# Layer 0's end put into an explicit order, and ranks read from rows with VectorE's 32x32 block transposes

## The chip, the cores and the metric

The kernel runs on one core of one Trainium2 chip. Its time is the device time in microseconds (us) of one execution. Besides the timed runs there is one execution taken by the hardware profiler; all views of the profile come from it. Engines: PE is TensorE's matmul, PEld its weight load, DVE is VectorE, ACT is ScalarE, POOL is GpSimd, SP is SyncE, which issues most of the transfers.

## The reference

Four graph layers over N = 2708 nodes with 128 features and one dense float32 adjacency matrix A. Each adds its result to x after a layer norm and a ReLU.

```
h = relu(layernorm(x))
# layer 0: degrees, a first product, the four nearest nodes, a second product
d  = 1/sqrt(rowsum(A));  z = leaky_relu((d * (A @ (d*h))) @ W1 + b1, 0.1)
S  = exp(-|z_i - z_j| / 2), kept for the 4 largest of each row, else 0
A2 = S + A;  d2 = 1/sqrt(rowsum(A2));  x += (d2 * (A2 @ (d2*h))) @ W2 + b2
# layer 1: attention
XW = h @ W;  Z = leaky_relu(s_row[:,None] + s_col[None,:], 0.01);  den = exp(Z)
att = den / (A @ den);  x += A @ (att @ XW)
# layer 2
x += h @ W_self + (A @ h / clip(rowsum(A), 1)) @ W_neigh
# layer 3
x += relu((A @ h) @ K + bias)
```

Here s_row and s_col are products of XW with the two halves of a vector.

## The kernel before, in words

**Tiles.** The nodes are T = 22 tiles of 128, the last one (T-1) with TAIL = 20 rows. A arrives transposed; a chunk is one tile of its rows, 128 x 2708 float32, 1354 KB. Columns of a product are cut into NKB = 6 blocks (`KBS`, five of 512 and one of 148), which are also the six groups of tiles (`GROUPS`). PSUM has six accumulators `acc(0)` to `acc(5)` and two small buffers `ps`. Chunks go through four `big` buffers and five `res` buffers, the latter for the last five tiles.

**Order of the work.** The program is written in order, but a scheduler chooses the order on each engine; `pin` fixes an instruction in program order among the pinned ones. SP issues the chunk loads in program order (they are pinned), and each waits until its buffer is free.

**Layer 0.** First the column sums of the chunks are taken on PE, with the layer norm's products `weighted` between them. `aggregate(y1, to_z)` is the first product with A. Each strip of similarities (one tile against all nodes) is then computed on PE, copied by ACT, and searched by DVE with MAX8 and FIND_INDEX8. For the last four strips (`LATE = T - 4`) the index is looked up later, in `find_last`. From the similarities come `dinv2`, the scaled rows `y2`, and their copy in DRAM, `ydr`, from which `add_near` gathers each tile's four neighbours: one indirect DMA of POOL for each of the four, and one DVE instruction that adds it to `xs`.

The second product is `aggregate(y2, done_l0)`: 17 chunks stream, then the tail, then the five resident chunks block by block. After a block is complete, `done_l0` turns it (`to_x1`), adds it to x, normalizes, adds late neighbours and computes terms of layer 1. `r_nat` holds one number for each node in the layout of the tiles, `row_all` the same numbers as a row on all partitions.

**Layer 1's ranks.** Node j's rank is the count of nodes i with `r_i >= r_j` and i before or at j in the order of ties. `place(t)` compares tile t with the nodes behind it (`mask`), counts by matmuls with ones into rows of `cnt`, and treats the tile's own 128 columns apart (`own_tiles`: less-or-equal minus ties under the diagonal). The remaining count (`later`) comes from a sum over the mask on ACT or DVE. `places_of(b)` brings a group's counts from a row of `cnt` to partitions: a copy, then four matmuls with a single partition, into `cn`. POOL scatters the group's nodes to `order_d` with one indirect DMA per tile. Between these, `total` multiplies each chunk by `w_n`; 9 chunks are resident then, 13 are loaded again. The sorted list `srtT` is loaded and turned on PE, and `fetch` gathers rows of A in this order by indirect DMA for the knots, a running sum over sorted rows, written to `table` in DRAM. Then rows are fetched from `table`, interpolated, and multiplied. Layers 2 and 3 are further calls of `aggregate`.

Of the kernel before, what the change touches and what calls it, by code (L numbers as in the profile page):

```python
# [25 lines left out]
def kernel(  # L26
# [46 lines left out]
    def pin(ins):  # L73

        return tc.keep_in_program_order(ins)

# [99 lines left out]
    one_b = ones_b[:, 0:1]  # L176
# [20 lines left out]
    def acc(b):  # L197
        return ps_a.tile([P, 512], F32, name=f"acc{b}")

# [166 lines left out]
    for i in range(T):  # L366
        c = chunk(i)
        w = width(i)
        if 3 <= i < 3 + 3 * NG:
            weighted((i - 3) // 3, i % 3)  # L370
        for b, (k0, n) in enumerate(KBS):
            g = 32 * (b % 4)
            nc.tensor.matmul(
                sums[b // 4][g : g + 32, :n],
                ones[:w, :32],
                c[:w, k0 : k0 + n],
                start=(i == 0),
                stop=(i == T - 1),
            )
        if i < FIRST:  # L380
            del resident[i]
    sum_rows = lay.tile([P, 1024], F32, name="sum_rows", tag="U")
# [112 lines left out]
    LATE = T - 4  # L495
# [3 lines left out]
    def strip(t):  # L499
        if LATE <= t < LATE + 2:  # L500
            return lay.tile([P, N], F32, name=f"strip{t}", tag="UZ"[t - LATE])
# [67 lines left out]
    nc.scalar.activation(dinv2, deg2s, AF.Exp, scale=-0.5)  # L569
    y2 = lay.tile([P, T, D], F32, name="y2", tag="Y")  # L570
    ydr = dram.tile([P * T, D], F32, name="ydr")
    for i in range(2):
        resident[i] = chunk(i)
    for t0, t1 in ((0, T // 2), (T // 2, T)):
# [14 lines left out]
    for t in (T - 2, T - 1, *range(LATE, T - 2)):  # L589
        find_last(t)  # L590
# [9 lines left out]
    def add_near(t, late=False):  # L600
        w = width(t)
        for k in range(TOPK):
            g = res.tile([P, D], F32, name="gath", bufs=23)
            nc.gpsimd.indirect_dma_start(  # L604
                out=g[:w, :],
                out_offset=None,
                in_=ydr[:, :],
                in_offset=bass.IndirectOffsetOnAxis(ap=near_u[:w, t, k : k + 1], axis=0),
            )
            term = nc.vector.scalar_tensor_tensor(  # L610
                xs[:w, t, :],
                g[:w, :],
                simd[:w, t, k : k + 1],
                xs[:w, t, :],
# [3 lines left out]
            if late and k == 0:  # L618
                pin(term)
# [34 lines left out]

# [20 lines left out]
    def last_terms(g):  # L675

        t0, t1 = GROUPS[g]
        k0, n = KBS[g]
        prod = res.tile([P, 4, D], F32, name="prod")
        nc.vector.tensor_tensor(  # L680
# [4 lines left out]
        )  # L685
        e = min(t1, T - 1)
        nc.vector.tensor_reduce(r_nat[:, t0:e], prod[:, : e - t0, :], AX.X, ALU.add)
        if e < t1:
            nc.vector.tensor_reduce(
                r_nat[:TAIL, e:t1], prod[:TAIL, e - t0 : t1 - t0, :], AX.X, ALU.add  # L690
            )
        p = ps_s.tile([P, 512], F32, name="ps")
        for t in range(t0, t1):
            w = width(t)
            o = (t - t0) * P
            nc.tensor.transpose(
                p[:, o : o + w], r_nat[:w, t : t + 1].to_broadcast([w, P]), ident[:w, :w]
            )
        return nc.scalar.copy(row_all[:, k0 : k0 + n], p[:, :n])
# [13 lines left out]
    def own_tiles(g, pool):  # L713
        t0, t1 = GROUPS[g]
        for c0, c1, w in ((t0, min(t1, T - 1), P), (max(t0, T - 1), t1, TAIL)):
            n = c1 - c0
            if n <= 0:
# [3 lines left out]
            eq = pool.tile([P, 4, P], BF16, name="eq", tag="spare")[:w, :n, :w]  # L721
            pin(nc.vector.tensor_tensor(eq, rows_, mine, ALU.is_equal))
            nc.vector.tensor_tensor(
                eq, eq, tri[:w, None, :w].to_broadcast([w, n, w]), ALU.mult
            )
            o = own[:w, c0:c1, :w]
            nc.vector.tensor_tensor(o, rows_, mine, ALU.is_le)
            nc.vector.tensor_tensor(o, o, eq, ALU.subtract)


    late = {0: (15,), 1: (16,), 2: (17,), 3: (18, 19), 4: ()}

    def done_l0(g, s2):
        to_x1(g, s2)
        if g < NG - 1:
            layernorm_relu(h1, g)
            for t in late[g]:
                add_near(t, late=True)
        if 1 <= g < NG - 1:
            terms(g - 1)  # L740
        if g == NG - 1:
            last_terms(g - 1)
        if g > 2:
            column_terms(g - 3)
        if g in (2, 3):
            own_tiles(g - 2, res)
# [3 lines left out]
    aggregate(y2, done_l0, lambda i: spread(y2, nc.sync) if i == 4 else None, kept=4)  # L750
    transposed(hT, h1, NG - 2, nc.scalar.copy)
    column_terms(NG - 3)
    for t in range(GROUPS[-1][0], T):
        add_near(t, late=True)
    layernorm_relu(h1, NG - 1)
    last_row = last_terms(NG - 1)
    transposed(hT, h1, NG - 1, nc.scalar.copy)
    column_terms(NG - 2)
# [17 lines left out]
    cnt, cn = (acc(2), acc(3)), (acc(4), acc(5))  # L776
# [10 lines left out]
    rmax = node_max("rmax", r_nat, r_ps[0][:, 256:384])  # L787
    r_n = vec("r_n")
# [24 lines left out]
    def place(t):  # L813
# [4 lines left out]
        def count(mask, c0, c1, first):  # L818
# [5 lines left out]
                ones_b[:w, :32],  # L824
                mask,
                start=(t == 0 and first),
                stop=(c1 == e and c1 in (512 * b + 512, N)),
            )

        count(own[:w, t, :w], a, e, True)  # L830
        if e < N:
            mk = flags.tile([P, N], BF16, name="mask")
            if t in (2, 6):
                nc.vector.tensor_scalar(
                    mk[:w, e:],
                    row_all[:w, e:],
                    rt,
                    0.0,
                    op0=ALU.is_le,
# [538 lines left out]
```

## Time and profile before

| | us |
|---|---|
| timed, median of 3 | 1194.0 |
| timed, lowest to highest | 1188.3 to 1194.6 |
| profiled execution, own time | 1289.2 |
| its span | 1287.3 |
| PE busy in the span | 1056.8 |
| DVE busy | 561.4 |
| ACT busy | 409.7 |
| POOL busy | 245.7 |
| mean granted TensorE clock | 0.902 of full speed |

The page gives busy time by engine, then the span in 40 slices, DMA queues, the chain that ended last and the costliest groups of instructions. A busy PE is not PE at its peak: a float32 matmul is two passes, and each pass takes twice as long at half clock. A timeline row has its start, its duration, the engine, the line in the code, the operation with output and inputs, and in brackets how long the engine had been idle and what ended that ("issue" is nothing that the profile shows). A table of stretches has, for each, the length, the busy time of PE, PEld, DVE, ACT and POOL with counts, the granted clock, the DMA engines' share and GB/s.

### The profile page before, as it was taken

The numbers are of one execution on the slowest core, as the hardware profiler recorded it, in microseconds if no ns is written. First come the engines' busy times: TensorE is split into PE (matmuls) and PEld (weight loads), VectorE is DVE, ScalarE is ACT, GpSimd is POOL, SyncE is SP. The second block draws the span as 40 slices with busy tenths as digits, with TensorE's granted clock in tenths as the row PEclk, the third lists the DMA queues.
The fourth block names the chain that finished last, engine by engine and source line by source line (L and its number), as shares of the span: only waits on it lengthen the run. The fifth ranks groups of instructions, "written<-read, shape, count | busy, mean of one in ns | idle before, by whom it ended". The sixth has DMA issues, their size and how long they took to land. (4 is left out here: it accounts for less than half of the span.)

```text
span 1287.3 us, 10181 instructions
## 1 busy us (share of the span) xinstructions
PE 1056.8 (82%) x3603; PEld 499.3 (39%) x3603; DVE 561.4 (44%) x1177; ACT 409.7 (32%) x636; POOL 245.7 (19%) x211
## 2 busy tenths in 40 slices
PE   4879999999763379797677771787879999999998
PEld 1324444444221134454333330333334445545444
DVE  2020026999832001783466663899970012104003
ACT  3100014544300000475567644687840012003000
POOL 4000000000277700134211103577500000000000
PEclk9989999999875579788899896698889999999999
DMA  9997800001553361256999997999949945761841
GB/s 344 422 383 276 302 3 1 1 1 43 212 202 96 94 253 50 90 233 245 274 406 395 345 348 269 423 414 419 417 184 395 326 164 181 265 245 54 306 159 43
DMA packets 38800, 298.76 MB, mean 232 GB/s; under 512 B 6735, under 2 KB 9710, under 8 KB 12290
## 3 DMA queue, kind: packets, MB, share of 16 engines
q1 hardware_dynamic: 24798, 203.76, 42.0%
q0 software_dynamic: 13952, 94.36, 19.7%
q8 instruction: 28, 0.46, 0.1%
q14 instruction: 22, 0.18, 0.0%
HBM read 265.76 MB, written 32.87 MB: 232 GB/s over the span
## 5 line engine op out<-in xcount | busy, mean ns | idle before, releaser
L284 PE MATMUL acc<-chunk,y 128*128 128x512 f32 (+1 forms) x408 | 180.3, 591 | 74.7 <-issue 58.4
L1213 PE MATMUL acc<-hi,xw 128*128 128x512 f32 (+3 forms) x264 | 124.2, 634 | 57.8 <-DVE hi L1203 57.8
L1106 PE MATMUL acc<-mov,wt 128*128 128x512 f32 (+1 forms) x264 | 115.4, 592 | 40.7 <-DMA mov<-in_adj_dram,src_u 39.2
L284 PE MATMUL acc<-chunk,h 128*128 128x512 f32 (+1 forms) x384 | 148.3, 542 | 0.0
L604 POOL DMA_INDIRECT gath<-ydr,near_u x88 | 83.8, 952 | 337.5 <-DMA ydr<-y 245.9
L284 PEld LDWEIGHTS acc<-chunk,y 128*128 128x128 f32 x408 | 79.5, 205 | 175.5 <-issue 162.0
L512 PE MATMUL acc<-zT 128*128 128x512 f32 (+2 forms) x264 | 112.7, 559 | 0.4 <-ACT strip L527 0.3
L1213 PEld LDWEIGHTS acc<-hi,xw 128*128 128x128 f32 (+1 forms) x264 | 55.7, 220 | 126.3 <-issue 66.1
L1110 DVE COPY mov<-acc 2x512 f32<-2x512 f32 x126 | 74.3, 611 | 61.1 <-PE acc L1106 60.5
L284 PEld LDWEIGHTS acc<-chunk,h 128*128 128x128 f32 x384 | 68.6, 190 | 73.2 <-issue 73.1
L1106 PEld LDWEIGHTS acc<-mov,wt 128*128 128x128 f32 x264 | 52.1, 205 | 103.8 <-issue 82.3
L527 ACT COPY strip<-acc 128x512 f32<-128x512 f32 (+2 forms) x132 | 60.7, 556 | 61.0 <-issue 35.8
L284 PE MATMUL acc<-chunk,attended 128*128 128x512 f32 x192 | 73.1, 542 | 2.5 <-DMA chunk<-in_adj_dram 2.5
L1145 POOL DMA_INDIRECT lo<-table,lo_u x22 | 58.0, 2638 | 68.6 <-issue 41.1
L1111 ACT COPY knots<-acc 128x512 f32<-128x512 f32 x88 | 50.2, 590 | 62.9 <-DVE mov L1110 56.4
L1195 ACT ACTIVATE hi<-hi,lam 128x2708 f32<-128x2708 f32 (+3 forms) x24 | 56.5, 2363 | 35.6 <-issue 26.7
L1191 DVE SCALAR_TENSOR_TENSOR hi<-lo,lam,hi 128x2708 f32<-128x2708 f32 (+3 forms) x24 | 67.1, 2801 | 1.0
L1203 DVE SCALAR_TENSOR_TENSOR hi<-row_all,inv_s,hi 128x2708 f32<-128x2708 f32 (+3 forms) x24 | 67.0, 2797 | 0.4 <-ACT hi L1196 0.4
L512 PEld LDWEIGHTS acc<-zT 128*128 128x128 f32 (+1 forms) x264 | 45.0, 185 | 51.7 <-issue 41.9
L529 DVE MAX8 top_v<-strip 128x8 f32<-128x2708 f32 (+1 forms) x22 | 64.4, 2967 | 0.4 <-ACT strip L527 0.4
L650 ACT COPY u2T<-acc 128x512 f32<-128x512 f32 (+1 forms) x6 | 3.2, 533 | 168.3 <-PE acc L284 168.2
L1196 ACT ACTIVATE hi<-hi,hb 128x2708 f32<-128x2708 f32 (+3 forms) x24 | 56.5, 2361 | 0.7
(281 smaller groups left out, 1179.5 us busy)
## 6 DMA issues: line engine op xcount, KB each, us to landing
chunk<-in_adj_dram SPq DMA_DIRECT2D x108, 1354.0 KB
table<-knots SPq DMA_DIRECT2D x20, 1354.5 KB
res<-in_adj_dram SPq DMA_DIRECT2D x9, 1354.0 KB
chunkY<-in_adj_dram SPq DMA_DIRECT2D x2, 1354.0 KB
chunkU<-in_adj_dram SPq DMA_DIRECT2D x2, 1354.0 KB
res<-in_adj_dram SPq DMA_DIRECT2D x8, 211.6 KB
ydr<-y SPq DMA_DIRECT2D x2, 704.0 KB
gath<-ydr,near_u POOLq DMA_INDIRECT x88
```

Of the source, the lines that this page charges most:

```text
L284: nc.tensor.matmul(out[b][:, :n], y[r, i, :], chunk(i)[r, k0 : k0 + n], start=(i == 0), stop=(i == T - 2),)
L512: mm = nc.tensor.matmul(zz[b][:w, :n], zT[:, cols(t)], zT[:, k0 : k0 + n], start=True, stop=False)
L527: copied = nc.scalar.copy(s[:w, k0 : k0 + n], zz[b][:w, :n])
L529: nc.vector.max(top_v[:w, t, :], s[:w, :])
L604: nc.gpsimd.indirect_dma_start(out=g[:w, :], out_offset=None, in_=ydr[:, :], in_offset=bass.IndirectOffsetOnAxis(ap=near_u[:w, t, k : k + ...
L1106: nc.tensor.matmul(p[:, :n], wt[:, t, :], moving[t][:, k0 : k0 + n], start=True, stop=True)
L1110: nc.vector.tensor_copy(moving[t + 1][:2, k0 : k0 + n], p[:2, :n])
L1145: nc.gpsimd.indirect_dma_start(out=dst[:w, :], out_offset=None, in_=table[:, :], in_offset=bass.IndirectOffsetOnAxis(ap=idx[:w, t : t + 1] ...
L1191: nc.vector.scalar_tensor_tensor(num, lo[:w, c], kap, num, op0=ALU.mult, op1=ALU.add)
L1195: nc.scalar.activation(num, num, AF.Ln, scale=sc)
L1203: nc.vector.scalar_tensor_tensor(att[:w, c], row_all[:w, c], inv_s[:w, t : t + 1], att[:w, c], op0=ALU.max, op1=ALU.mult,)
L1213: nc.tensor.matmul(py[b][:, :n], xw[:w, t, :], att[:w, k0 : k0 + n], start=(t == T - 1), stop=(t == T - 2),)
```

## The change

It has these parts.

- `warm` issues bf16 matmuls of 128x512 whose result nobody reads: three after each of the last six chunks of the sums, 16 ahead of the second product, 14 ahead of the knots. In the sums the 20-row tile T-1 goes before T-2.
- `LATE` is T-5. Three of the late strips take the places of resident chunks 17 to 19, which are loaded again during the second product; four chunks instead of two are loaded ahead of it. `ydr` is written in three parts.
- Layer 0's end is written out through `Ordered`, which pins every instruction of PE, DVE and ACT: the last two blocks are completed first, and then turned, added and normalized in one sequence. The 20-row tile's neighbours come from one gather on four strips of partitions, added up by one matmul. Its indices and factors are spread by eight small DMAs on ACT's queue. Groups 3, 4 and 5 get their terms by row sums on DVE, and are transposed after the maximum of `r_nat`.
- `own_tiles` has two instructions instead of four, and keeps only the ties. `place` compares from the tile's own columns on, and takes the ties off by a matmul with minus one.
- `places_of` uses four 32x32 block transposes on DVE per group instead of the copy and the matmuls.
- Two `total` fewer stand between the counts.

```diff
+    def warm(p, n):
+        for _ in range(n):
+            pin(
+                nc.tensor.matmul(
+                    p, ident_b, ident_b[:, None, :].to_broadcast([P, 4, P]), start=True, stop=True
+                )
+            )
...
-    for i in range(T):
+    for n_, i in enumerate([*range(T - 2), T - 1, T - 2]):
...
+        if n_ >= T - 6:
+            warm(acc(0), 3)
...
-    LATE = T - 4
+    LATE = T - 5
...
     def strip(t):
-        if LATE <= t < LATE + 2:
-            return lay.tile([P, N], F32, name=f"strip{t}", tag="UZ"[t - LATE])
+        if t in (LATE, T - 2, T - 1):
+            i = T - L0_RES + (LATE, T - 2, T - 1).index(t)
+            del resident[i]
+            return res_rows.tile([P, N + 1], F32, name=f"strip{t}", tag=f"res{i}")[:, :N]
+        if t > LATE:
+            return lay.tile([P, N], F32, name=f"strip{t}", tag="UZ"[t - LATE - 1])
...
+    warm(acc(5), 16)
...
-    for i in range(2):
+    for i in range(4):
         resident[i] = chunk(i)
-    for t0, t1 in ((0, T // 2), (T // 2, T)):
+    for t0, t1 in ((0, 9), (9, 17), (17, T)):
...
+    for k in range(TOPK):
+        for dst, src in ((near_p, near_u), (simd_p, simd)):
+            nc.scalar.dma_start(dst[32 * k : 32 * k + TAIL, :], src[:TAIL, T - 1, k : k + 1])
...
+    def last_near():
+        g = gathered(near_p)
+        dve.tensor_scalar(four_w, four_w, simd_p, None, op0=ALU.mult)
+        p = ps_s.tile([P, 512], F32, name="ps")
+        pe.matmul(p[:TAIL, :P], four_w[:, :TAIL], g, start=True, stop=True)
+        return p
...
-            pin(nc.vector.tensor_tensor(eq, rows_, mine, ALU.is_equal))
-            nc.vector.tensor_tensor(
-                eq, eq, tri[:w, None, :w].to_broadcast([w, n, w]), ALU.mult
-            )
             o = own[:w, c0:c1, :w]
-            nc.vector.tensor_tensor(o, rows_, mine, ALU.is_le)
-            nc.vector.tensor_tensor(o, o, eq, ALU.subtract)
+            pin(nc.vector.tensor_tensor(o, rows_, mine, ALU.is_equal))
+            nc.vector.tensor_tensor(o, o, tri[:w, None, :w].to_broadcast([w, n, w]), ALU.mult)
...
     def done_l0(g, s2):
+        if g >= NG - 2:
+            complete.append(s2[g])
+            return
         to_x1(g, s2)
-        if g < NG - 1:
-            layernorm_relu(h1, g)
-            for t in late[g]:
-                add_near(t, late=True)
...
+    column_terms(0)
+    add_near(T - 3, dve)
+    x1(E4)
+    for t in range(*GROUPS[E4]):
+        moments(t)
+    roots(E4)
+    x1(E5)
+    normed(E4)
+    p = last_near()
+    prod = row_sums(E4 - 1)
+    natural(E4 - 1, prod)
+    as_row(E4 - 1)
+    column_terms(1)
+    column_terms(2)
+    dve.tensor_tensor(xs[:TAIL, T - 1, :], xs[:TAIL, T - 1, :], p[:TAIL, :P], ALU.add)
+    moments(T - 1)
+    add_near(T - 2, dve)
+    moments(T - 2)
+    roots(E5)
+    prod = row_sums(E4)
+    normed(E5)
+    natural(E4, prod)
+    as_row(E4)
+    natural(E5, row_sums(E5))
+    last_row = as_row(E5)
...
+        for b, (k0, n) in enumerate(KBS):
+            c0, c1 = max(a, k0), k0 + n
+            if c0 < c1:
+                count(c0, c1, ones_b, mk[:w, c0:c1], t == 0, False)
+        count(a, e, minus_b, own[:w, t, :w], False, e == N or e % 512 == 0)
...
-        mine = spare.tile([P, 512], F32, name="mine", bufs=2)
-        nc.vector.tensor_copy(mine[g : g + 1, :n], cnt[b // 4][g : g + 1, :n])
-        for t in range(t0, t1):
-            w = width(t)
-            o = (t - t0) * P
-            nc.tensor.matmul(
-                cn[b % 2][:w, t : t + 1],
-                mine[g : g + 1, o : o + w],
-                ones[g : g + 1, :1],
-                start=True,
-                stop=True,
-            )
+        mine = spare.tile([P, 4, 32], F32, name="mine", bufs=2)
+        rows_ = cnt[b // 4][g : g + 32, :].rearrange("p (t f) -> p t f", f=P)
+        for r in range(0, P, 32):
+            m = sum(r < width(t) for t in range(t0, t1))
+            nc.vector.transpose(mine[r : r + 32, :m, :], rows_[:, :m, r : r + 32])
...
-        if 1 <= t <= len(here) + 4 or t in (15, 16, 18, 20):
+        if 1 <= t <= len(here) + 4 or t in (16, 19):
             total(done)
             done += 1
...
     weights(0)
+    warm(acc(5), 14)
```

## The prediction

> **What bounds the kernel now.** I read the page's slices first, then busy time by stretch with borders at the stage changes (sums of rows, first product, similarities, second product, layer 0's end, ranks, knots, rows, the last three products), then the timeline at each border.
>
> ```profile
> 93.00:205.00 112.00, 110.50 (x323) 52.68 (x324) 17.36 (x52) 10.33 (x42) 1.57 (x3) 0.97 0.50 177
> 205.00:337.00 132.00, 122.17 (x409) 50.23 (x407) 124.86 (x91) 64.45 (x150) 0.00 (x0) 0.98 0.06 22
> 337.00:501.00 164.00, 100.35 (x208) 42.21 (x212) 35.14 (x88) 3.96 (x10) 79.10 (x83) 0.71 0.47 169
> 501.00:552.00 51.00, 41.61 (x166) 24.14 (x161) 30.39 (x127) 19.46 (x45) 4.67 (x5) 0.81 0.16 57
> 552.00:612.00 60.00, 51.44 (x513) 29.95 (x513) 35.99 (x84) 39.52 (x58) 24.55 (x24) 0.85 0.63 256
> 612.00:800.00 188.00, 125.44 (x352) 62.07 (x352) 104.77 (x234) 109.31 (x150) 34.66 (x32) 0.88 0.93 338
> 944.00:1287.00 343.00, 333.49 (x1026) 166.34 (x1026) 63.85 (x264) 38.41 (x77) 4.62 (x9) 0.99 0.59 212
> ```
>
> Each line gives the stretch and its length, busy us of PE, PEld, DVE, ACT and POOL, then granted clock, DMA share and GB/s. The first and the last product stages are PE-bound, the similarities PE and DVE together, the knots DMA-bound. Three stretches are bound by none of these: 337 to 501, 501 to 552, 552 to 612. The change works on them.
>
> 337 to 501 is special. Its timeline on PE:
>
> ```profile
> 398.81 1.01 PE L284 MATMUL acc<-chunk,y 128*128 128x512 f32 x1 [1.80 <-issue]
> 401.62 1.01 PE L284 MATMUL acc<-chunk,y 128*128 128x512 f32 x1 [1.80 <-issue]
> ```
>
> From 370 to 457 PE starts a pass every 2 to 3.5 us and waits for nothing that the profile shows, while POOL issues a gather each 1.256 us. A chunk costs 4.545 us undisturbed (the last aggregates: 36.36 us for 96 passes, 12 a chunk), so 17 chunks are 77.3 us, with 2 us for the cold start; they took 163.4 (337.3 to 500.7). About 84 us are stall. The profiled run is 1289.2 us (span 1287.3 and 1.9 around it), the timed runs 1188.3 to 1194.6: the stall can't be in these. Without it the profiled run gives 1205, 11 over the median. So the sum is made on the trace less 84 us, and the gain is taken from 1194.0. On this shortened scale the chunks end at 416.6, and layer 0 (`row_all` complete) at 552.25 - 84 = 468.2.
>
> **What the Trainium skill says.** "TensorE: Matmul & The Clock Gate", Part 1: the array runs at half clock until about 3.4 us of sustained activity. The trace agrees: granted clock 0.50 after waits, a 128x512 pass 0.85 us instead of 0.43. Same page, Part 2: matmuls stay in program order, only weight loads are pulled ahead. Here it shows as counts that queue behind a `total` (L913) whose chunk is in flight. "DMA: Bandwidth & Descriptors", Anatomy of one DMA: about 2 us fixed. The trace has 4.2 us from the end of the second `ydr` issue (340.0) to the first gather (344.2), transfer included. "VectorE: DVE Perf Modes", The three transpose paths: VectorE transposes 32x32 blocks only, 311 ns for 128x128 bf16. No run here shows it yet.
>
> **The change, part by part.**
>
> 1. *Sums.* The 20-row chunk goes before the last full one, and 18 bf16 passes (128x512) keep PE active. Before, 24 passes follow the last wait:
>
> ```profile
> 84.85 5.38 PE L373 MATMUL ps<-res,ones 128*32 128x512 f32 x24 [3.13 <-DMA res<-in_adj_dram]
> ```
>
> They run at 0.50 to 0.85 clock; 12 warm ones take 1.9 us (row at 79.07). With the 20-row load (0.5 us) now ahead, the end moves from 90.2 to 87.5 to 88.7. The first product then starts at 93.51, cold until about 99: up to 2.5 us more if the clock holds across the 1.8 us gap, which it didn't before. The warming costs 0.64 us a chunk; PE was busy 17 of 20 us, so 0 to 1.2 us comes back. Range -5 to 0; I take -2.5.
>
> 2. *Similarities.* `LATE` from T-4 to T-5 takes one FIND_INDEX8 (2.98 + 0.08 us) out of the DVE row that ends at 334.36. ACT's last strip copy ends at 328.9, so MAX8 of the last tile moves from 331.4 to 328.9 and no further: -2.5 us. The index runs later, under the product. The price is three chunks loaded again (4.06 MB, 9.6 us at 424 GB/s): 16 loads at 3.2 us plus gathers (0.2 of the DMA) in 77 us of products; with four chunks loaded early (SP: two more loads ahead of `ydr`, whose buffers are free by then) PE has 18 us of lead. I cost it at nothing; a shortfall would show as PE waits on chunks, up to 10 us.
>
> 3. *Start of product 2.* PE waited 9.6 us and ran cold from 337.3 to 341.2, 2 us lost. 16 warming passes end at about 332.4, 2.4 us before y2. Gain 0 to 2. `ydr` in three writes: the last is 0.32 MB instead of 0.70, about 1 us less, partly eaten by a third issue (0.33 us). Gathers start at 341, against 344.2.
>
> 4. *Layer 0's end.* PE's last product is at 528.84, `row_all` is complete at 552.25: 23.4 us of short steps in each other's way, PE at half clock. In it DVE shows:
>
> ```profile
> 537.13 0.16 DVE L673 COPY r_nat<-acc 128x4 f32<-128x4 f32 x1 [1.91 <-PE acc L670]
> 539.46 0.35 DVE L644 SCALAR_TENSOR_TENSOR xs<-ps,dinv,xs 128x128 f32<-128x128 f32 x1 [1.97 <-PE ps L262]
> 543.17 0.69 DVE L680 TENSOR_TENSOR prod<-h,wrow 128x512 f32<-128x512 f32 x1 [1.71 <-ACT h L221]
> 551.97 0.28 ACT L699 COPY row_all<-ps 128x148 f32<-128x148 f32 x1 [1.63 <-PE ps L696]
> ```
>
> Afterwards these steps stand in one order. The tail's four gathers become one (85 instead of 88, 3.8 us of POOL), one small matmul and an add; its eight small DMAs sit in ACT's queue under the product, where ACT idles. In the order, everything of the last groups queues on DVE behind tile T-3's gathers. The 80th gather issues at 341 + 79 x 1.256 = 440.2 and lands near 443.4; PE's last product is at about 412 + 27 = 439. So gathers decide. From 443.4: last term 0.3, x1 1.1, moments 1.3, tile T-1 and T-2 of x1 0.5, root, reciprocal and factor 0.9, products and sums of group 3 1.5, tail add and moments 0.6: 449.6; T-2's gathers land about 449.8, terms 0.3, moments 0.4, root to h 1.8, sums of the last group 1.2, transposes and copy 0.9: 454.5. Against 468.2: -13.7, parts 2 and 3 contained. If the order waits worse than I see, -6; if gathers land earlier, -17.
>
> 5. *Ranks.* `row_all` to first fetch is 552.25 to 611.71, 59.5 us. The fetch waits for the transposes of the sorted list, which stand behind all `total` matmuls on PE:
>
> ```profile
> 592.00:596.00 4.00, 0.50 (x4) 0.43 (x3) 1.30 (x5) 1.06 (x3) 1.23 (x2) 0.72 1.03 419
> 598.85 7.57 PE L913 MATMUL ps<-chunk,w_n 128*32 128x338 f32 x65
> 610.17 0.29 PE L1006 MATMUL acc<-ident,srtT 22*126 22x22 f32 x1
> 611.71 1.11 POOL L1015 DMA_INDIRECT mov<-in_adj_dram,src_u  x1 [4.16 <-DVE kn L1043]
> ```
>
> The chunks stream at 419 GB/s from 560 and are in by 597; then five totals are left, 11.2 us partly cold, because PE waited for chunks with counts behind them. Moving two totals behind the counts removes that. `w_n` comes 0.9 us later (three ACT copies of 0.59, 0.59, 0.28 us go before it), the stream of 11 chunks takes its 35 us, one total follows: about 46 us, then 2 us to the fetch. The other chain must keep pace: DVE was busy 34.3 us in 552 to 600. Own tiles go from 6.1 to 5.2, masks add 128 columns each (22 x 0.077 = 1.7 and 0.2), six `mine` copies (3.7) leave, and 24 block transposes come, unknown here: at least 0.14 (the cheapest small DVE row), 0.68 at most (the 1x512 copy they replace); I take 0.3, near the page's 311 ns: 7.2. That makes 38.8, plus 2.6 for two scatters and 4.5 for the list's load: 46, the same as the stream. The 44 matmul passes into `cn` (6.8 us, 5.8 waited) vanish; the minus-one products and longer masks add some 30 short bf16 passes, under the stream. Fetch at +48 to +51: I take -10. At 0.68 a transpose it is -2.
>
> 6. *Knots.* 14 warming passes run while PE waits 6.5 us for the first rows. First passes were cold (7.16 us), but DMA is 1.00 busy from 616: -0.5 (-2 to +1). Starting earlier moves the whole later program, since no later stage changes.
>
> Sum: -2.5 - 13.7 - 10 - 0.5 = -26.7: 1194.0 becomes 1167, and the profiled run, if it stalls alike, about 1262.
>
> **Rivals.**
> - *Half of it*: timed runs lack 11 us of the reconstruction; if these lie in the two short stages, or transposes cost 0.5 us and more, ranks give 2 to 5 and layer 0's end 8: 1178 to 1184. For it: balance of DVE chain and stream. Against: PE's backlog is plain.
> - *More*: clock held at both warmings and gathers cheaper without the profiler: -35, 1159 or below, to 1148.
> - *Slower*: the 32x32 transposes from PSUM on DVE become the bound. Past 0.3 us each, every 0.1 us adds 2.4 us. The ranks lose all their own gain at 0.7 us and all 26.7 us at 0.3 + 26.7 / 24 = 1.4 us; at 2 us the kernel takes 1208. Against: 128 elements a partition is a small DVE instruction, and such rows here take 0.2 to 0.35 us.
> - *It doesn't do what it says*: the clock falls in spite of warming. Costs 3 us of the gain, in the range.
>
> **Chances.** A measurement can tell about 0.5% (6 us). Likeliest 0.58 (its own range 1158 to 1177); half 0.20; more 0.10; within 0.5%, gains lost to new waits, 0.06; slower 0.06. Range 1148 to 1186.
>
> **What would show it.** Right: `row_all` complete within about 14 us of PE's last product; fetch 48 to 51 us later; no five totals in a row after the chunks; StreamTranspose rows near 0.3 us; clock near 1.0 at the first passes of both products. Wrong: PE waits on `chunk` or `res` in product 2; DVE full to the end of the ranks with transposes over 0.7 us; a gap before x1 longer than the gathers explain.

## The result, and the profile after

The changed kernel takes 1188.55 us (median of 20 runs, 1183.8 to 1196.9) against 1192.45 us (20 runs, 1188.3 to 1196.4) of the kernel before: ratio 0.997, interval 0.9952 to 0.9987, a gain of about 4 us. The forecast was 27 us. The profiled execution takes 1185.9 us (span 1184.2), 2.7 below its median; the profiled execution of the kernel before stood 97 us above its own.

First the stage table of the kernel after, borders at product 2, at PE's last chunk of it, at the complete `row_all` and at the first fetch (busy us of PE, PEld, DVE, ACT, POOL, then clock, DMA share, GB/s):

```profile
330.30:417.00 86.70, 79.67 (x204) 37.33 (x204) 37.72 (x89) 3.68 (x10) 60.84 (x64) 0.98 0.84 321
417.00:460.00 43.00, 37.13 (x154) 21.59 (x154) 26.82 (x119) 18.52 (x44) 20.17 (x22) 0.86 0.31 99
460.00:513.50 53.50, 45.80 (x490) 23.59 (x489) 39.40 (x99) 39.75 (x59) 24.48 (x24) 0.85 0.71 287
```

The one long stretch of before, 337 to 501 at a DMA share of 0.47, is now 330.3 to 417: there is no stall in this profile. What PE does in it is in the timeline:

```profile
339.48 18.34 PE L306 MATMUL acc<-chunk,y 128*128 128x512 f32 x48
360.73 9.33 PE L306 MATMUL acc<-chunk,y 128*128 128x512 f32 x24 [2.91 <-DMA chunk<-in_adj_dram]
372.81 11.02 PE L306 MATMUL acc<-chunk,y 128*128 128x512 f32 x24 [2.75 <-DMA chunk<-in_adj_dram]
385.19 32.04 PE L306 MATMUL acc<-chunk,y 128*128 128x512 f32 x84 [1.36 <-DMA chunk<-in_adj_dram]
```

Instead of 1.8 us of "issue" before each pass there are three waits on chunks, 7.0 us together. The product starts 7.0 us earlier than in the profile before (330.29 for 337.28; 5.0 of these are the kernel's, as the mean over all profiles shows further on) and the chunks end at 417.2, where the shortened trace of before had 416.6: the lead is gone by then.

The end of layer 0 and of the ranks, from the same timeline:

```profile
442.62 0.94 POOL L647 DMA_INDIRECT gath<-ydr,near_u  x1 [0.30 <-DVE xs L699]
444.19 0.41 PE L306 MATMUL acc<-res,y 128*128 128x148 f32 x2
459.62 0.28 ACT L84 COPY row_all<-ps 128x148 f32<-128x148 f32 x1 [0.79 <-PE ps L84]
...
472.86 1.27 DVE L1002 STREAM_TRANSPOSE mine<-acc 32x128 f32<-32x128 f32 x4 [2.17 <-PE acc L961]
499.02 5.91 PE L1047 MATMUL ps<-chunk,w_n 128*32 128x338 f32 x78
508.99 1.88 PE L1047 MATMUL ps<-chunkY,w_n 128*32 128x338 f32 x16 [2.12 <-DMA chunkY<-in_adj_dram]
509.88 0.58 POOL L1139 DMA_DIRECT2D srtT<-order_d  x1 [1.59 <-DMA order_d<-pay,to_u]
513.43 1.09 POOL L1150 DMA_INDIRECT mov<-in_adj_dram,src_u  x1 [2.98 <-DVE kn L1178]
```

Read with the lines of before: from PE's last product to the complete `row_all` it is 15.3 us (444.6 to 459.9), where it was 23.4. The four block transposes take 1.27 us, 0.32 each. From `row_all` to the first fetch it is 53.5 us for 59.5; two chains end it within a microsecond: PE's last total (510.9, which waited for its chunk) and POOL's row of 22 scatters, whose list is loaded at 509.9.

So the two profiles differ by much more than 4 us: the stalled trace less 84 us has its first fetch at 527.7, the profile after at 513.4. The experiments ask why the timed runs do not show these 14 us.

### The profile page after: what moved, and what is told of

It reads as the page before. It is cut to its first block, busy times and chain, and to the rows that moved or that the text cites. A ratio compares the mean times of both kernels' runs of the same rounds, so it can differ in the third digit from the quotient of the medians.

```text
span 1184.2 us, 10223 instructions
## 1 busy us (share of the span) xinstructions
PE 1028.3 (87%) x3613; PEld 487.6 (41%) x3613; DVE 561.7 (47%) x1190; ACT 408.9 (35%) x636; POOL 241.3 (20%) x208
## 5 line engine op out<-in xcount | busy, mean ns | idle before, releaser
L1349 PE MATMUL acc<-hi,xw 128*128 128x512 f32 (+3 forms) x264 | 119.0, 610 | 60.9 <-DVE hi L1339 60.9
L306 PE MATMUL acc<-chunk,y 128*128 128x512 f32 (+1 forms) x408 | 157.4, 547 | 11.1 <-DMA chunk<-in_adj_dram 7.0
L647 POOL DMA_INDIRECT gath<-ydr,near_u x84 | 80.1, 953 | 265.7 <-DMA ydr<-y 240.5
L306 PEld LDWEIGHTS acc<-chunk,y 128*128 128x128 f32 x408 | 74.0, 191 | 94.7 <-issue 90.4
L1349 PEld LDWEIGHTS acc<-hi,xw 128*128 128x128 f32 (+1 forms) x264 | 53.5, 211 | 126.4 <-DVE hi L1339 64.0
L1247 ACT COPY knots<-acc 128x512 f32<-128x512 f32 x88 | 50.0, 589 | 57.4 <-DVE mov L1246 53.5
L1109 ACT ACTIVATE sg<-row_all,c_nat 128x2708 bf16<-128x2708 f32 (+1 forms) x22 | 56.2, 2556 | 0.1
```

What stands on the lines that cost most here:

```text
L306: nc.tensor.matmul(out[b][:, :n], y[r, i, :], chunk(i)[r, k0 : k0 + n], start=(i == 0), stop=(i == T - 2),)
L647: nc.gpsimd.indirect_dma_start(out=g[: idx.shape[0], :], out_offset=None, in_=ydr[:, :], in_offset=bass.IndirectOffsetOnAxis(ap=idx, axis=0),)
L1349: nc.tensor.matmul(py[b][:, :n], xw[:w, t, :], att[:w, k0 : k0 + n], start=(t == T - 1), stop=(t == T - 2),)
```

## Experiments

Times are medians; ratios are against the kernel before on the same chip.

**The kernel before, profiled again.** No edit.

> The kernel before, unchanged, for a second profile. Theory one (the prediction's failed step is the shortened trace): without the stall of PE in product 2 the kernel before is itself shorter by about 11 us than the stalled trace less 84 us. Then the span is 1188 to 1195, product 2 starts near 337, and row_all is complete before 468, or the first fetch comes less than 59.5 us after it. Rival: the borders are those of the shortened scale (chunks end 416.6, row_all 468.2, fetch 527.7) and the span is near 1203; then the profile of the changed kernel is the odd one. If the stall comes again, the span is near 1287 and nothing is decided.

The stall was there again (span 1284.1), and in the timed runs too: 33 runs of the kernel before gave 1281.3 us on this chip. Two more profiles:

> The kernel before once more, for a profile without PE's stall in product 2 if this chip does not have it. If the base of the prediction was wrong, row_all is complete near 460 to 463 (the 88 gathers, 1.257 us apart from 344, end at 454 and set it) instead of 468.2, and the first fetch comes 59 us later, near 520. Rival: 468 and 527 as on the shortened scale, and the 11 us lie after the fetch, in the knots and rows (675.6 us from the fetch to the end in the first profile). On a chip with the stall: span near 1284 again.

> The kernel before a third time, in the hope of a chip on which PE does not stall in product 2. There: span 1187 to 1194, no wait of PE for issue between 365 and 455, the 88 gathers 1.25 us apart in one row to about 454, row_all complete near 460 to 465. On a chip with the stall: span 1284 to 1291, row_all near 551.

Spans 1290.9 and 1286.3, timed 1283.7 and 1282.7, on two other chips. PE in the second of the three:

```profile
339.37 30.29 PE L284 MATMUL acc<-chunk,y 128*128 128x512 f32 x76
370.16 0.59 PE L284 MATMUL acc<-chunk,y 128*128 128x512 f32 x1 [0.51 <-issue]
373.66 0.59 PE L284 MATMUL acc<-chunk,y 128*128 128x512 f32 x1 [2.91 <-issue]
...
455.59 1.01 PE L284 MATMUL acc<-chunk,y 128*128 128x512 f32 x1 [1.09 <-issue]
456.99 5.90 PE L284 MATMUL acc<-chunk,y 128*128 128x512 f32 x10 [0.39 <-issue]
466.54 33.74 PE L284 MATMUL acc<-chunk,y 128*128 128x512 f32 x84 [3.65 <-DMA chunk<-in_adj_dram]
```

The stall is thus no accident of one profiled execution. There are chips that hold PE back in this stage, at every execution (four of those used here: medians of 1279 to 1284 us), and chips that don't (the one of the first comparison, 1192.45, and one further on, 1190.5). Each chip was met once, so the record does not separate the chip from anything else that stayed fixed while it was used, such as where the buffers lay. The profile before, by its stall, came from the first kind; the timed runs beside it, by their 1188 to 1195 us, from the second. In what follows they are called holding chips and free chips.

**The kernel after on a chip that holds PE back.** No edit.

> The kernel after, on the same chip as the others of this set. Without the stall: near 1188, 4 us below the kernel before. With the stall in it (timed runs of before near 1281): if the change's gain does not depend on the stall, about 4 us (1277); if the traces are right that layer 0's end and the ranks are 8 and 6 us shorter wherever the gathers are done before PE's last product, 13 to 18 us (1263 to 1268).

1266.5 us against 1283.7: ratio 0.985 (0.981 to 0.989), a gain of 17 us; the second guess held. Here the change is worth some four times what it is worth on the free chip. Its trace against the last one shown: PE's last product ends at 515.0 instead of 528.3, `row_all` is complete at 530.3 instead of 551.6, the fetch comes at 588.7 instead of 610.9. The stall costs 54.0 us of issue waits in 30 places, for 59.5 in 33; the other profiles with the gathers at their own pace have 54.6 to 59.9, before and after alike, so the stall itself is no shorter. In the eight profiles with all gathers from two holding chips, POOL issues 83 gathers in one row, and PE's last single stalled pass comes 7 to 12 us after the row's last gather (447.8 and 455.6 in the profile above; 440.1 and 452.1 after). The row ends 7.7 us earlier after, the stall 3.5 us, and the product starts 7.0 us earlier. Not all of the 13 us at PE's last product belong to the change: in the run below that changes the ranks alone, whose code up to there differs from that of before by a few VectorE instructions only, the product starts at 334.0 and ends at 520.3.

**Half the gathers.** Two neighbours of four, and memsets on POOL in the gap:

```
+    idle_p = res.tile([P, P], BF16, name="idle_p")
+
+    def idle():
+        for _ in range(5):
+            pin(nc.gpsimd.memset(idle_p, 0.0))
...
-        for k in range(TOPK):
+        for k in range(TOPK // 2):
...
-            nc.gpsimd.indirect_dma_start(
+            pin(nc.gpsimd.indirect_dma_start(
...
+            idle()
```

> Before, with half of layer 0's gathers left out (two neighbours of four; the output is another) and about 1.1 us of POOL memsets put behind each remaining gather, so that POOL's row of work in product 2 is as long as before with half the transfers. If the stall of PE comes from the dense row of gathers, it shrinks or vanishes on a chip that has it: the time falls from about 1282 to below 1240, to about 1190 if it is gone; then this is a picture of the kernel before without the stall. Rival: the stall belongs to PE's own work in this stage and has nothing to do with the gathers; then the time stays within 10 us of 1282.

> After, with the same half of the gathers left out and the same memsets. If without the stall the change is worth 4 us, as on the chip of the first comparison, this is 3 to 6 us below its partner; if the 15 to 19 us that it is worth on a chip with the stall do not come from the stall, it is 15 us below it.

1196.5 us for the kernel before with this edit, on a chip where it takes 1282.7 without, and 1188.0 for the kernel after. The stall is gone:

```profile
339.68 74.24 PE L284 MATMUL acc<-chunk,y 128*128 128x512 f32 x196
413.85 9.04 PE L284 MATMUL acc<-res,y 20*128 20x512 f32 x28
```

196 passes in a row where the unthinned kernel has 33 waits for issue. The stall belongs to the dense row of gathers; PE's own work is unchanged. And the pair differs by 8.5 us (single runs 1195.0 to 1197.1 and 1185.6 to 1192.7), which fits neither of the two expected values, 3 to 6 and 15. The end of `row_all`, first before, then after:

```profile
461.83 0.28 ACT L708 COPY row_all<-ps 128x148 f32<-128x148 f32 x1 [1.84 <-PE ps L705]
```

```profile
457.12 0.28 ACT L84 COPY row_all<-ps 128x148 f32<-128x148 f32 x1 [0.79 <-PE ps L84]
```

So `row_all` is complete at 462.1 and 457.4 (on the shortened trace it was 468.2). PE's last product is at 441.3 and 442.0, although product 2 starts at 334.4 and 331.6: the lead of 2.8 us at the start is given back here too. The first fetch is at 521.8 and 516.3.

**Gathers further apart, none left out.** One memset behind each gather in the kernel after, then two in both kernels (the kernel after then with its reloads from chunk 12 on):

```
+        for _ in range(1):    # 2 in the other two
+            pin(nc.gpsimd.memset(idle_p, 0.0))
```

> After, with all gathers and one POOL memset of 0.26 us behind each, so that the gathers stand 1.35 to 1.5 us apart instead of 1.257. If the stall of PE hangs on the closeness of the gathers, it shrinks: below 1250 on a chip where after takes 1266. If it hangs on the number of transfers in flight or on the bytes, the row of gathers is longer, the stall lasts as long as the row does, and the time is 1266 or up to 20 us above it.

1248.1 us, ratio 0.974 (0.970 to 0.978). The kernel after has 0.985 (0.981 to 0.989) on such a chip: 14 us by the ratios, 18 by the medians of two chips. The gathers stand 1.39 us apart instead of 1.25 (83 from 337.9 to 452.2), and PE's waits for issue fall to 35.2 us:

```profile
385.66 1.01 PE L306 MATMUL acc<-chunk,y 128*128 128x512 f32 x1 [1.80 <-issue]
388.44 1.94 PE L306 MATMUL acc<-chunk,y 128*128 128x512 f32 x2 [1.78 <-issue]
390.60 1.01 PE L306 MATMUL acc<-chunk,y 128*128 128x512 f32 x1 [0.21 <-issue]
392.00 1.26 PE L306 MATMUL acc<-chunk,y 128*128 128x512 f32 x2 [0.40 <-issue]
```

Some passes now come in twos, with short waits between. The row of gathers grew by 12 us and the stall shrank, so closeness decides, not length. On this holding chip the kernel is faster than before and, by the ratios, than after.

> After, all gathers, two POOL memsets (0.25 us each) behind each gather, so some 1.6 us apart, and the reloads from chunk 12 on. With one memset the gathers stood 1.39 us apart and 18 us were gained on a chip with the stall. If the stall ends at a spacing below 1.6 us, the row of gathers (85 x 1.64 = 139 us, to about 477) sets layer 0's end near 492 and the time is 1214 to 1222; if it only shrinks in proportion, 1225 to 1245; if the longer row costs more than the stall gives, above 1248.

> Before, with the same two memsets behind each gather. If the stall goes, the row of 88 gathers from 341 to 344 ends near 486 and the time is 1228 to 1240 (was about 1282 on such a chip), some 10 to 16 us above its partner: 5 us for four gathers less and an earlier start, 6 to 8 for the ranks. If it only shrinks, 1240 to 1262.

These two met a free chip (kernel before 1190.5 us), so they say nothing of the stall, and there the longer row of gathers (1.86 us apart after, 1.89 before) makes them slow: 1228.7 and 1236.6, 38 and 46 us above the kernel before. But they gave what no other run had, the ranks of before on a free chip. POOL's last gather, the complete `row_all` and the first fetch, first the kernel before with two memsets, then the kernel after with them:

```profile
507.98 0.90 POOL L611 DMA_INDIRECT gath<-ydr,near_u  x1 [0.56 <-DVE own L736]
514.44 0.28 ACT L708 COPY row_all<-ps 128x148 f32<-128x148 f32 x1 [1.63 <-PE ps L705]
567.45 1.11 POOL L1024 DMA_INDIRECT mov<-in_adj_dram,src_u  x1 [2.88 <-DVE tots L1041]
```

```profile
496.53 0.96 POOL L654 DMA_INDIRECT gath<-ydr,near_u  x1 [0.49 <-DVE xs L84]
504.03 0.28 ACT L84 COPY row_all<-ps 128x148 f32<-128x148 f32 x1 [0.79 <-PE ps L84]
557.70 1.09 POOL L1159 DMA_INDIRECT mov<-in_adj_dram,src_u  x1 [2.90 <-DVE kn L1187]
```

From `row_all` to the fetch: 52.7 us before (514.7 to 567.4), 53.4 after (504.3 to 557.7), and 53.5 in the first profile after. In these profiles, one each, the new ranks are no shorter than the old on a free chip. And from the start of the last gather to `row_all`: 6.7 us before, 7.8 after. Where the gathers decide layer 0's end, the explicit order does not shorten it; the 10.4 us between the two borders come from the row of gathers, which starts 3.7 us earlier, has three gathers fewer and ends 11.4 us earlier.

**The ranks alone, and without.** Into before: minus-one products, block transposes, totals at 16 and 19. Out of after: the reverse, in the full kernel and in the half-gather kernel.

```
-        if 1 <= t <= len(here) + 4 or t in (15, 16, 18, 20):
+        if 1 <= t <= len(here) + 4 or t in (16, 19):
```

With it go `place`, `places_of` and `own_tiles` of the other kernel.

> Before, with the ranks' part alone (minus-one products, block transposes, two totals less among the counts). If the gain of 6 us that the two traces show between row_all and the first fetch is real, the time is 1185 to 1187; if it belongs to the stalled trace, or w_n and the chain of scatters set the end of the ranks in both kernels, it is within 2 us of 1192.

> After, with the old ranks put back (counts turned by matmuls, ties taken off on VectorE, totals at 15, 16, 18, 20). The sums, similarities, start of product 2 and layer 0's end stay new. If the ranks' part is the larger half of the 4 us, it is 1190 to 1192; if the ranks' part is worth 6 us and the rest costs 2, it is 1194 or more; if the rest is what pays, about 1188.

> The same half-gather kernel after, with the ranks of before put back. If the new ranks are worth the 6 us that the first comparison of profiles showed, it is 5 to 7 us above its partner (1188); if only the 1 us that the two half-gather kernels show between row_all and the fetch (59.7 and 58.9), within 2 us of it; if they cost, below it.

1276.0 us, ratio 0.996 (0.994 to 0.998): 5 us better than before. 1268.0, ratio 0.991 (0.988 to 0.994): 13 us better than before without the new ranks; beside 0.985 for the whole change, but on another chip and with intervals that touch. In the half-gather kernel the old ranks (there with 22 gather buffers instead of 23) cost 8 us: 1195.5 (ratio 0.9345, 0.931 to 0.938), where two kernels with the new ranks, timed beside it and told of below, have 1186.5 and 1187.4 (0.928, 0.923 to 0.934). The intervals still overlap a little. With the old ranks this kernel is level with the half-gather kernel before (0.933, 0.930 to 0.936): without the stall, the rest of the change gives nothing that shows in the time. All three ran on holding chips. There the ranks suffer too, even where product 2 has no stall: in the half-gather kernel before they take 59.7 us. Seven microseconds each, the same place after `row_all`, first the kernel before on such a chip (its second repeat):

```profile
580.00:587.00 7.00, 5.28 (x56) 2.82 (x48) 3.24 (x13) 2.44 (x6) 3.72 (x4) 1.00 1.01 417
587.00:594.00 7.00, 7.00 (x44) 3.61 (x44) 2.00 (x11) 2.22 (x9) 3.88 (x4) 0.51 1.01 420
```

then the same code on the free chip (the kernel before with two memsets):

```profile
543.10:550.10 7.00, 6.98 (x95) 4.50 (x88) 4.85 (x22) 4.40 (x13) 5.04 (x6) 1.00 1.01 417
550.10:557.10 7.00, 5.68 (x53) 3.31 (x52) 3.59 (x15) 5.50 (x10) 4.83 (x5) 0.85 1.02 418
```

With DMA as full as there and POOL scattering, PE gets through 100 passes instead of 148 and its clock falls to 0.51. That is the backlog of totals which the prediction saw. On the free chip totals stand in a row at the end too (555.2 to 565.0), but they no longer set it: the transposes of the sorted list wait 0.92 us more, for the list's load. What slows PE in the ranks of the holding chips was not separated from the waits on DVE that the slices also hold.

**The reload.** Four late tiles and two early chunks as before, so that no resident chunk is loaded twice; or the three reloads later:

```
-    LATE = T - 5
+    LATE = T - 4
...
-    for i in range(4):
+    for i in range(2):
         resident[i] = chunk(i)
```

```
-    aggregate(y2, done_l0, lambda i: spread(y2, nc.sync) if i == 4 else None, kept=4, back=5)
+    aggregate(y2, done_l0, lambda i: spread(y2, nc.sync) if i == 4 else None, kept=4, back=12)
```

The first edit is that of the two runs without reload (with it go the strips and the order of `find_last` of the kernel before).

> After, with four late tiles and two early chunks as before, so that no resident chunk is dropped and loaded again. If the reload's transfers cost the 7 us of waits on chunks in product 2, those waits fall below 1 us, the chunks end near 412 to 414 though the product starts 2.5 us later, and the time is 1183 to 1186. Rival: gathers and DVE set layer 0's end whatever the chunks do; then the chunks end earlier, row_all stays near 460, and the time is 1188 or, by the longer similarities, 1190.

> The same half-gather kernel after, with four late tiles and two early chunks as before, so no reload. Similarities end 2.5 us later and product 2 starts near 334; if the earlier start of gathers is what counts, 2.5 to 4 us above its partner; if the reload had given all of the lead back, the time is the same within 1 us.

> After, with the three reloads issued from chunk 12 on instead of chunk 5. If they are what made PE wait 7 us on chunks in product 2, those waits fall below 2 us and the chunks end near 410 instead of 417.2. If PE's last product then decides layer 0's end, row_all is complete near 454 and the kernel gains 4 to 6 us against after; rival, the gathers (last one issued at 442.6) decide, row_all moves by less than 2 us and the time is that of after within 2 us.

> The kernel after with half of the gathers left out and memsets behind the rest (as the earlier run of that kind), and the three reloads from chunk 12 on. Without PE's stall the 3.1 us of waits on chunks should vanish and PE's last product end near 439 instead of 442. If PE's last product sets layer 0's end there, row_all is complete near 454 (was 457.4) and the time is 3 us lower; rival: the row of gathers sets it, row_all stays within 1 us of 457 and so does the time.

On holding chips nothing shows in the time: 1268.4 (ratio 0.990, 0.987 to 0.994) and 1263.4 (0.983, 0.979 to 0.987), neither told apart from the 0.985 of after. In the half-gather kernels, where PE is not stalled, the mechanism shows. With the reloads from chunk 5 on, two profiles have 2.5 and 5.5 us of waits on chunks (the kernel after and the one with the old ranks). With the reloads from chunk 12 on:

```profile
337.69 72.00 PE L306 MATMUL acc<-chunk,y 128*128 128x512 f32 x190
409.62 9.04 PE L306 MATMUL acc<-res,y 20*128 20x512 f32 x28
```

No wait is left, and PE's last product ends at 437.1 instead of 442.0 (5 us, more than expected). But `row_all` is complete at 456.6 instead of 457.4: the row of gathers, last issued at 446.3, decides (DVE waits 5.2 us for gathers there), and the time, 1186.5 us, is that of its partner on another chip (1188.0). Without the reload product 2 starts at 334.1, has 1.7 us of waits and takes 1187.4 in all: again the same, as far as four runs between 1182 and 1195 can tell. What the reload buys at the start it spends on the way.

**Warming left out.**

```
-        if n_ >= T - 6:
-            warm(acc(0), 3)
-    warm(acc(5), 16)
-    warm(acc(5), 14)
```

> After, without its 48 warming passes. The prediction gave them 1 to 4 us together (sums 1 to 2.5, start of product 2 up to 2, knots 0.5): expected 1 to 4 us slower than after. Rival: the warming costs as much as it brings (0.64 us for each of the last six chunks, and a lower clock later on), and the time is that of after within 1 us, or below it.

1263.8 us, ratio 0.985 (0.980 to 0.989), that of after: the rival fits better, though these intervals can't exclude a gain of 1 or 2 us. At the end of the sums, first without warming, then the kernel after:

```profile
85.01 3.11 PE L396 MATMUL ps<-res,ones 128*32 128x512 f32 x12 [0.18 <-DMA res<-in_adj_dram]
```

```profile
85.40 0.82 PE L217 MATMUL acc<-ident_b 128*128 128x512 bf16 x3
86.15 1.90 PE L396 MATMUL ps<-res,ones 128*32 128x512 f32 x12
```

The last twelve passes are 1.2 us shorter when warm and, in these two profiles, start 1.1 us later, behind the warming itself. The first half agrees with the Trainium skill ("TensorE: Matmul & The Clock Gate", Part 1: half clock until the array has been active for some 3.4 us); the second is the price of the warming where the work behind it is this short.

What the warming was for is the start of the products. The first 6 us of the first product, in the kernel before, without warming, and after:

```profile
93.51:99.51 6.00, 6.00 (x8) 2.56 (x9) 2.64 (x5) 0.00 (x0) 1.57 (x3) 0.56 0.68 218
```

```profile
91.78:97.78 6.00, 6.00 (x10) 2.57 (x11) 2.64 (x5) 0.00 (x0) 1.57 (x3) 0.72 0.81 283
```

```profile
91.69:97.69 6.00, 6.00 (x16) 2.89 (x17) 2.65 (x5) 0.00 (x0) 1.57 (x3) 1.00 0.88 327
```

Sixteen passes at full clock instead of eight or ten: in the profile after the clock holds across the gap of 1.8 us. It does so in 5 of the 12 profiles with warming, with the same gap in all, and the first product is then 1.7 us shorter (101.1 for 102.8). At product 2 it holds in 8 of the 10 in which the gap is 2.3 us, and in neither of the two without reload, where it is 4.7 us. None of the eight profiles without warming has more than eleven passes there.

**The best guess at that point.** Reloads from chunk 12 on, and `w_n` ahead of ACT's three copies:

```
-    for g in range(E4 - 1, NG):
-        transposed(hT, h1, g, nc.scalar.copy)
     r_n = vec("r_n")
...
+        pin(nc.scalar.activation(w_n, r_n, AF.Exp, scale=0.01))
+    for g in range(E4 - 1, NG):
+        transposed(hT, h1, g, act.copy)
```

> After, with the reloads from chunk 12 on, and w_n computed on ACT ahead of the three copies of transposed h1 (0.59, 0.59, 0.28 us), which the totals don't need. w_n should come 4.7 us after row_all instead of 6.0, the stream of chunks start 1.3 us earlier, and the first fetch come 1 to 1.5 us earlier counted from row_all; with the reloads, 1 to 6 us below after. Rival: POOL's row of 22 scatters, 1.28 us apart, sets the fetch, and nothing moves by more than 0.5 us.

1266.2 us, ratio 0.985 (0.981 to 0.990): no gain over after on a holding chip. `w_n` came 3.5 us after `row_all` (535.6 after 532.1) instead of 6.0, and the fetch 61.2 us after it: its totals waited 3.8 us for issue in 5 places, those of after on such a chip 2.0 in 3. Whether it gains on a free chip wasn't tried.

## Why the prediction was wrong

The forecast was 1205 - 26.7 = 1178.3 on the profile's scale. The timed kernel after took 1188.55, 10.2 us more, and the base that stood for the kernel before, 1205, was 12.5 above its timed 1192.45. The two make the 22.8 us between -26.7 and -3.9. Up to the first fetch the profile after misses the forecast by 11.9 us (513.4, where 527.7 less 2.5, 13.7 and 10 is 501.5): 7.9 up to `row_all` and 4.0 in the ranks. Behind the fetch it is 4.8 us shorter than the first profile (670.8 for 675.6), although nothing there changed but part 6; over all twenty profiles this stretch takes 667 to 680 us, so some of the agreement or disagreement of totals is chance.

*The base: the step "Without it the profiled run gives 1205 ... So the sum is made on the trace less 84 us".* It took the stalled passes out and left all else of that trace as it was. But the chip that stalls PE in product 2 also slows it in the ranks: `row_all` to fetch is 59.5 us there and 52.7 on a free chip, 6.8 us. And `row_all` itself, 468.2 on the shortened scale, is at 462.1 where the stall is removed by half the gathers, 6.1 us (an estimate for the full kernel, since half of its gathers are missing and no unthinned trace of before from a free chip exists). Together 12.9, about the 12.5 to be found, but that they fit so closely is luck. Of the 6.1 us, 2.9 are an earlier start of product 2 in that profile (334.4 for 337.3), which also came on a holding chip with all gathers (334.0, the run with the ranks alone). And the profiled executions of the kernel before are long ones of their kind: the three repeats stand 4.6, 9.1 and 5.4 us above the medians of their chips, and the four take 673 to 680 us from the first fetch to the end, where the two in which nothing stalls take 673.6 (half the gathers) and 667.6 (two memsets, free chip). How much of the 12.5 is the chip and how much the single execution was not separated. The rival "half of it" named these 11 us and where they might lie; it was given 0.20 and should have led, and even it kept too much of the ranks.

*Part 5, ranks, -10.* The mis-sized term is PE's backlog. The price of the transposes was right: 0.32 us for 0.3 forecast, close to the 311 ns that the Trainium skill gives ("VectorE: DVE Perf Modes", The three transpose paths) for the other shape, 128x128 bf16. But the fetch came 53.5 us after `row_all`, not 48 to 51, and the old ranks need 52.7 on a free chip. Of the chain of 22 scatters, 1.27 us each and the last 14 without a gap, only two stood in the sum; with the stream of chunks it holds the end where it was. The part gains 5 to 8 us on holding chips and, by the profiles, nothing on free ones.

*Part 2, reload "at nothing".* It cost 7.0 us of waits on chunks in the profile after, and 1.9 us more at a lower clock behind the second of them (24 passes in 11.0 us, where two chunks need 9.1); the text had named exactly this as the sign and up to 10 us as its size. The similarities' own -2.5 came as forecast: from PE's last small product among the similarities to `sim` it was 7.09 us (327.30 to 334.39) and is 4.59 (322.82 to 327.41). The lead reached product 2 and ended there.

*Part 4, layer 0's end, -13.7.* "Gathers decide" was right for an undisturbed product: first gather at 337.0, earlier than the 341 assumed, last at 442.6. With the waits of part 2, though, PE's last product came at 444.6 instead of 439, and the ordered steps then take 15.3 us: `row_all` at 459.9 instead of 454.5. The saving from 23.4 to 15.3 is real where PE is late, on holding chips; where the gathers are last, the steps behind them take 7.8 us in the new order and 6.7 in the old.

*Parts 1 and 3, warming.* At the end of the sums the -2.5 is not there: their transposes start at 89.1 us in the mean of seven profiles with the old order (87.1 to 90.3) and at 88.8 in that of the twelve with new order and warming. The single line of before that the step rested on was a late one. It came one stage later, where the text had only put a chance: the first product ends at 196.2 in the mean of the seven (194.0 to 197.5) and at 193.8 in that of the twelve (192.8 to 195.9), 2.4 us earlier. With the similarities' 2.5 this makes a lead of 5.0 us at product 2 (331.3 for 336.2, without the two kernels that have no reload). The size was right; part 2's waits took it away.

*Part 6.* No effect seen: without any warming the time is the same within the interval.

What was right: the direction, the price of the transposes, the similarities, the clock near 1.0 at the start of both products in the profile after, and the sign by which the reload would show. On a holding chip the change gains 17 us, two thirds of the 26.7 and inside the range: the forecast was nearer for the kind of chip that was profiled than for the kind that was timed.

Still open: what in the holding chips differs; and whether the kernel after with reloads from chunk 12 on gains on a free chip. There PE's last product should come 5 to 7 us earlier; with 15.3 us behind it, 7.8 to 10.3 us behind the last gather, and the later of the two deciding, `row_all` would be complete near 453 to 455 instead of 459.9, an estimate. It was run on holding chips alone.

## What to carry to other kernels

Where the profiled execution is far from the timed runs, as here by 97 us, the trace may show another chip than the timing: subtracting the visible stall does not give the trace of the timed kernel, and what looks like backlog in later stages may be the same disturbance. Get a profile whose own time agrees with the median, or remove the disturbance by an edit, before pricing stages from it; and repeat a border in several profiles before building 2 us on it. Prefetching that loads the same bytes again was not free here until it was issued when DMA had room: in the half-gather kernel three loads of 1.35 MB issued seven chunks later left no wait. And a warmed clock is a chance, not a term to add in full: over the same gap it held in some executions and not in others.

## What the runs showed of the hardware

- On four of the chips met here (kernel before 1279 to 1284 us), the row of indirect gathers, issued 1.25 us apart on POOL, keeps TensorE from issuing: 33 waits with 59.5 us in all in one profile, around passes at a low clock, some 84 us of a 1285 us kernel. At 1.39 us apart it is 35.2 us, at 2.6 us apart with half the gathers nothing. On the free chip that was profiled at 1.25 (kernel after, 1188.55 us) there is none; the other free chip shows it by its time alone (1190.5).
- The start of the stall trails the first gather by 24 to 35 us; the last single stalled pass trails the row's last gather by 7 to 12 us.
- A memset of 128x128 bf16 behind each gather, 0.23 us, made the kernel after 14 to 18 us faster on a holding chip; with two of them both kernels took 38 to 46 us more than the kernel before on a free one.
- After warming passes and an idle gap of 1.8 us, TensorE kept its full clock in 5 of 12 profiles; after one of 2.3 us in 8 of 10; after 4.7 us in neither of two.
